# Two hyperbolic graph layers: full-row products and degree 4 against paired half-row products, degree 3 and ends from dot products

## The chip, the core and the metric

The kernel runs on one core of a Trainium2 chip. The metric is the device time of one execution in microseconds (us); lower is better. The core has five engines with a queue each: TensorE (PE, its weight loads shown apart as PEld), VectorE (DVE), ScalarE (ACT), GpSimd (POOL) and SyncE (SP, which here only issues transfers).

## What is computed

Four graph layers are applied to `x` (3327 nodes, 64 features, float32) with a dense 0/1 matrix `adj` (3327 x 3327). Each layer normalises `x` over its features, takes the positive part `h`, and adds the layer's output to `x`. Layers 0 and 3 are the hyperbolic ones, and only they change:

```python
x_t = logmap0(h, c)
left, right = x_t @ w[:64], x_t @ w[64:]
adj_att = sigmoid(left[:, None] + right[None, :] + b) * adj
x_local = logmap(h[:, None, :], h[None, :, :], c)      # all pairs of nodes
support = einsum('ij,ijd->id', adj_att, x_local)
x = x + proj(expmap(h, support, c), c)
```

`logmap` and `expmap` go through `mobius_add`, `artanh` and `tanh`; c is 1 in layer 0 and 1/r^2 in layer 3. Layer 1 is a sum over neighbours with decaying weights, layer 2 a gated recurrent unit over sums of neighbours.

## The kernel before

Nodes are padded to 3328, that is T = 26 blocks of P = 128, so `[P, T, 64]` tiles hold one row per node (1664 numbers in a partition). The order of work is layer 0, layer 1 (`plain_decay`), layer 2 (`plain_gat`), layer 3, then a branch that is taken only if the inputs leave the range for which the fast formulas hold. A tile framework puts the instructions of each engine in an order at build time, from the dependences and the number of buffers of each tile, and it sets all semaphores; each engine then runs its queue in that order.

Both hyperbolic layers are `hyperbolic_series` (L235 to L390). All pairs (j, i) are worked off as a matrix of 3328 x 3328 weights: per pair, a polynomial in a quantity L that is an inner product of two prepared rows of length 65, times the attention weight. The function has three stages.

*Preparation* (L247 to L338). DVE makes `H` by `norm_relu`, the squared norms `x2`, and `rows` (64 features and one number per node). TensorE transposes `rows` to `LT` (65 x 3328) by `to_columns` (L108: four transposes into a PSUM tile, then one ACT copy); `RT` is `LT` with signs. A chain of small operations with square root and logarithm gives the scale of `logmap0`; the scaled `H` is transposed to `xtT`; TensorE then makes `left`, spread over all partitions (`leftB`, L333), and `right` (L337).

*Pair loop* (L340 to L379). Outer loop `c`: 4 chunks of W = 832 columns i. Inner loop `b2`: 13 pairs of blocks of j. In each pass ACT makes two sigmoids (L357, 832 wide), POOL multiplies them by the adjacency (L359, 1664 wide; in layer 0 from a float32 tile that SP loads, with the diagonal taken out by `drop_diagonal`; in layer 3 from float8 masks that layer 1 left in SBUF). Then for each of the two blocks:

```python
PE.matmul(L[:, h, :BK], LT[:, b*P:(b+1)*P], RT[:, ...], ...)      # L364, h = 0, 1; 65 rows, 416 columns
A.activation(y, Lu, AF.Square, scale=0.5, bias=g1_c)              # L368
A.activation(y, y, AF.Square, bias=g2_c)                          # L369
V.scalar_tensor_tensor(Lu, Lu, 0.5 * G3, y, ...)                  # L370
V.scalar_tensor_tensor(w, Lu, G4 - 0.5 * G3, sig[...], ...)       # L372
PE.matmul(acc[h], rows[:, b, :], w[:, h, :], ...)                 # L375, h = 0, 1; 65 output rows
```

The two sums `acc[0]` and `acc[1]` (65 x 416 each) collect all 26 blocks and are copied out by ACT (L379, one buffer each) at the end of a chunk. `L` has three buffers of two PSUM banks. `sig`, `y` and `w` have two buffers.

*End* (L381 to L390). TensorE turns the sums back into rows (`to_rows`, L124), DVE copies them to `M` (L383), and `move` (L149 to L233) does `expmap`, the addition in the ball and the projection with full `[P, T, 64]` operands: `dot` is a product (L153) and a sum (L155) over 1664 numbers, `axpby` two products and an addition (L162 to L164). The last one adds to `X` (L233).

Layer 1's loop (L882 to L916) is not changed but is used below: it alternates bfloat16 matmuls over the full array (L900, L904, 128 x 128) with pairs of matmuls whose outputs are 64 columns wide and go to the two halves of the output partitions (L909).

Of the kernel before, what the change touches and what calls it, by code (L numbers as in the profile page):

```python
# [9 lines left out]
F32 = mybir.dt.float32  # L10
BF = mybir.dt.bfloat16
# [7 lines left out]
P = 128  # L19
# [9 lines left out]
G0, G1, G2, G3, G4 = 0.30970640316, -0.36098355479, 0.46940675477, -1.28660460234, 2.86920527402  # L29
X2_MIN = 18.0  # L30
# [3 lines left out]
def tile_gnn4(ctx: ExitStack, tc: tile.TileContext, x, adjT, att0, b0, w1, bias1, w_gat, a_gat,  # L34
# [26 lines left out]
    g1_c = column(G1 - 0.5, "g1_c")  # L61
    g2_c = column(G2, "g2_c")
# [172 lines left out]
    def hyperbolic_series(att, b_att, r, min_norm, min_norm2, ok, masks=None):  # L235
# [8 lines left out]
        W = 2 * BK  # L244
        R = D + 1
        with ExitStack() as st:
            pers = st.enter_context(tc.tile_pool(name="hs", bufs=1))  # L247
            rows = pers.tile([P, T, R], F32, name="rows")
# [3 lines left out]
            LT = pers.tile([R, NP], F32, name="LT")  # L252
            RT = pers.tile([R, NP], F32, name="RT")
            leftB = pers.tile([P, NP], F32, name="leftB")
            right = pers.tile([P, T], F32, name="right")
            maxn2 = pers.tile([P, 1], F32, name="maxn2")
            um = pers.tile([P, 1], F32, name="um")
            isqc = None

            with tc.tile_pool(name="hsp", bufs=1) as tp, tc.tile_pool(name="hsps", bufs=2, space=PSUM) as ps:  # L260
                w_l = tp.tile([D, 1], F32, name="w_l")
                w_r = tp.tile([D, 1], F32, name="w_r")
                nc.sync.dma_start(w_l, att[:D])
                nc.sync.dma_start(w_r, att[D:])
                bcol = tp.tile([P, 1], F32, name="bcol")
                nc.scalar.dma_start(bcol, bcast_rows(b_att))
                w_lb = tp.tile([D, P], F32, name="w_lb")
                V.tensor_copy(w_lb, w_l.to_broadcast([D, P]))
# [6 lines left out]
                floor = tp.tile([P, 1], F32, name="floor")  # L275
                V.memset(floor, 1e-7)
                V.memset(maxn2, min_norm2)
                if r is None:
                    V.memset(um, min_norm)
                    V.tensor_copy(hs, H)  # L280
                else:
# [5 lines left out]
                    isqc = pers.tile([P, 1], F32, name="isqc")  # L287
                    V.reciprocal(isqc, sqc)
                    V.tensor_scalar(um, sqc, min_norm, None, op0=OP.mult)
                    V.tensor_scalar(maxn2, cc, min_norm2, None, op0=OP.mult)  # L290
                    V.tensor_max(floor, floor, maxn2)
# [7 lines left out]
                V.tensor_mul(rows[:, :, :D], hs, wide(ia))  # L299
                V.tensor_scalar(rows[:, :, :D], rows[:, :, :D], 2.0, None, op0=OP.mult)  # L300
                V.scalar_tensor_tensor(rows[:, :, D], x2, 1.0, ia, op0=OP.add, op1=OP.mult)


                z = tp.tile([P, T], F32, name="z")
                V.tensor_scalar(z, x2, floor, None, op0=OP.max)
                z = sqrt_(tp, z, "zs")
                zc = tp.tile([P, T], F32, name="zc")
                v = tp.tile([P, T], F32, name="zv")
                lu = tp.tile([P, T], F32, name="zlu")
                lv = tp.tile([P, T], F32, name="zlv")  # L310
                V.tensor_scalar(zc, z, CLIP, None, op0=OP.min)
                V.tensor_scalar(v, zc, -1.0, 1.0, op0=OP.mult, op1=OP.add)
                A.activation(lu, zc, AF.Ln, bias=one_c)
                A.activation(lv, v, AF.Ln)
                V.scalar_tensor_tensor(v, zc, 1.0, v, op0=OP.add, op1=OP.subtract)
                V.scalar_tensor_tensor(v, zc, 2.0, v, op0=OP.mult, op1=OP.subtract)
                V.tensor_sub(lu, lu, lv)
                V.tensor_add(lu, lu, v)
                V.reciprocal(z, z)
                V.scalar_tensor_tensor(z, lu, 0.5, z, op0=OP.mult, op1=OP.mult)  # L320
                xt = tp.tile([P, T, D], F32, name="ln_sq")
                V.tensor_mul(xt, H, wide(z))

                to_columns(ps, LT, rows, R)
                sgn = tp.tile([R, 1], F32, name="sgn")
                V.memset(sgn, 1.0)
                V.memset(sgn[:D], -1.0)
                V.tensor_scalar(RT, LT, sgn, None, op0=OP.mult)
                xtT = tp.tile([D, NP], F32, name="xtT")
                to_columns(ps, xtT, xt, D)  # L330
                for k in range(NP // BK):
                    pl = ps.tile([P, BK], F32, name="pl")
                    PE.matmul(pl, w_lb, xtT[:, k * BK:(k + 1) * BK], start=True, stop=True)  # L333
                    V.tensor_copy(leftB[:, k * BK:(k + 1) * BK], pl)
                pr = ps.tile([P, T], F32, name="pr")
                for t in range(T):
                    PE.matmul(pr[:, t:t + 1], xtT[:, t * P:(t + 1) * P], w_r, start=True, stop=True)  # L337
                V.tensor_scalar(right, pr, bcol, None, op0=OP.add)  # L338

            with tc.tile_pool(name="hsw", bufs=2) as wk, tc.tile_pool(name="hsps", bufs=3, space=PSUM) as ps, \  # L340
                    tc.tile_pool(name="hsacc", bufs=1, space=PSUM) as pa:
                for c in range(NP // W):
                    c0 = c * W
                    acc = [pa.tile([R, BK], F32, name=f"acc{h}") for h in range(2)]
                    for b2 in range(T // 2):
                        if masks is None:
                            adj = wk.tile([P, 2, W], F32, name="adj", bufs=4)
# [752 lines left out]
```

## Time and profile before

| what | value |
|---|---|
| median of three runs | 1274.11 us (1266.6 to 1274.59) |
| the profiled execution: its time | 1277.46 us |
| the profiled execution: its span | 1275.7 us |
| mean granted TensorE clock | 0.895 |
| layer 0: preparation, pair loop, end | 57.7, 337.6, 50.8 us |
| layer 1 and layer 2 | 253.9 and 140.0 us |
| layer 3: preparation, pair loop, end | 49.6, 327.4, 58.7 us (the last with the store) |

A line of a stage table has the stretch, its length, the busy time of each engine with its number of instructions, the granted TensorE clock (1 is full), and the share and rate of the transfers. A line of a group has the source line, the engine, the operation, output and inputs by name, the shapes, the number of instructions, then busy time and mean ns of one, then the idle time of the engine ahead of them with what ended it. A line of a timeline has start and length in us, engine, line, operation, shapes and how many consecutive ones are merged (x4).

### The profile page before, as it was taken

Reading aid. Unit: us, or ns where it says so; the run is one execution under the profiler, and the core shown is the slowest. Engines: PE = TensorE matmul, PEld = TensorE weight load, DVE = VectorE, ACT = ScalarE, POOL = GpSimd, SP = SyncE. Lnnn points to the kernel's source line nnn. Section 1 sums busy time; section 2 is a strip of 40 time slices with the busy share of each in tenths; the row PEclk is TensorE's granted clock in tenths of the full one; section 3 lists DMA queues with packets and bytes.
Section 4 is the critical chain, followed back from the end, with each engine's and each line's share of the span. In section 5 each row is a group of like instructions: output and inputs, shape, how many; then the busy total and the mean of one; then the engine's idle time right before and its main releaser. Section 6 shows DMA issues by size and latency. Waiting matters only on the chain.

```text
span 1275.7 us, 11381 instructions
## 1 busy us (share of the span) xinstructions
PE 997.5 (78%) x4051; PEld 477.7 (37%) x4051; DVE 823.7 (65%) x937; ACT 726.2 (57%) x851; POOL 393.6 (31%) x166
## 2 busy tenths in 40 slices
PE   0989999999993037888996699919899998999910
PEld 0634444344441032333332476406344443444400
DVE  7255666566668969994933402793466676667787
ACT  1378879889883013444453001413689999899910
POOL 0065665665661000201210000000445555455500
PEclk9789989999997568999999799966799999999965
DMA  2153444444420009992910000000000000000001
GB/s 28 57 171 121 134 134 134 134 136 135 139 101 0 0 21 341 302 305 82 297 47 9 6 2 1 1 0 1 0 1 1 0 1 1 0 1 1 0 3 28
DMA packets 41844, 91.62 MB, mean 72 GB/s; under 512 B 15152, under 2 KB 15152, under 8 KB 41776
## 3 DMA queue, kind: packets, MB, share of 16 engines
q1 hardware_dynamic: 37200, 90.76, 21.9%
q10 hardware_dynamic: 4576, 0.02, 0.3%
q8 instruction: 34, 0.56, 0.2%
q14 instruction: 34, 0.28, 0.1%
HBM read 89.92 MB, written 0.85 MB: 71 GB/s over the span
## 4 chain that ended last, share of the span: by engine, by line
PE 45%; DVE 22%; ACT 17%; POOL 7%; issue 6%; DMA 2%; ACTq 0%; DVEq 0%; POOLq 0%; SPq 0%
PE acc L375 13%; PE L L364 9%; POOL sig L359 7%; PE acc L909 6%; ACT y L369 5%; DVE w L372 5%; PE acc L974 4%; ACT w L902 4%; PE cnt L904 4%; ACT sig L357 3%; ACT y L368 3%; DVE L L370 3%; PE cnt L900 2%; PE pt L114 2%; DVE prod L153 1%
## 5 line engine op out<-in xcount | busy, mean ns | idle before, releaser
L375 PE MATMUL acc<-w,rows 128*65 128x416 f32 x832 | 341.3, 535 | 39.9 <-DVE w L372 38.1
L364 PE MATMUL L<-RT,LT 65*128 65x416 f32 x832 | 334.2, 527 | 0.7 <-DVE right L338 0.7
L370 DVE SCALAR_TENSOR_TENSOR L<-L,y 128x832 f32<-128x832 f32 x208 | 213.8, 1030 | 185.4 <-ACT y L369 181.7
L359 POOL TENSOR_TENSOR sig<-mask,sig 128x1664 f32<-128x1664 fp8e4 x52 | 164.6, 3167 | 385.2 <-ACT sig L357 375.1
L372 DVE SCALAR_TENSOR_TENSOR w<-L,sig 128x832 f32<-128x832 f32 x208 | 212.5, 1024 | 52.9 <-POOL sig L359 35.8
L368 ACT ACTIVATE y<-L,g_c 128x832 f32<-128x832 f32 x208 | 195.8, 943 | 76.5 <-PE L L364 76.5
L359 POOL TENSOR_TENSOR sig<-adj,sig 128x1664 f32<-128x1664 f32 x52 | 193.1, 3716 | 102.2 <-ACT sig L357 102.1
L364 PEld LDWEIGHTS L<-RT,LT 65*128 65x128 f32 x832 | 162.6, 196 | 149.9 <-issue 146.9
L369 ACT ACTIVATE y<-y,g_c 128x832 f32<-128x832 f32 x208 | 203.9, 983 | 3.5
L357 ACT ACTIVATE sig<-leftB,right 128x832 f32<-128x832 f32 x208 | 201.2, 977 | 7.5 <-DVE w L372 7.4
L375 PEld LDWEIGHTS acc<-w,rows 128*65 128x65 f32 x832 | 108.9, 141 | 242.7 <-DVE w L372 117.1
L902 ACT ACTIVATE w<-cnt,ebias 128x832 bf16<-128x832 f32 x104 | 93.7, 950 | 110.9 <-PE cnt L900 68.8
L146 POOL TENSOR_TENSOR mask<-mask,offdiag 128x128 fp8e4<-128x128 fp8e4 x26 | 23.4, 902 | 248.0 <-PE cnt L904 241.6
L895 DVE SCALAR_TENSOR_TENSOR same<-adj 128x1664 bf16<-128x1664 f32 x52 | 99.0, 1904 | 0.0
L909 PE MATMUL acc<-w,sup 128*64 128x416 bf16 x624 | 94.0, 349 | 0.0
L904 PE MATMUL cnt<-mask,rest 128*128 128x416 fp8e4 x208 | 54.1, 341 | 28.7 <-ACT w L902 28.7
L900 PE MATMUL cnt<-mask,after 128*128 128x416 fp8e4 x208 | 55.2, 350 | 9.7 <-DVE mask L892 9.7
L974 PE MATMUL acc<-mask,h 128*64 128x416 fp8e4 x624 | 60.9, 345 | 0.7 <-ACT hP L827 0.7
L909 PEld LDWEIGHTS <-sup 128*64 128x64 bf16 x624 | 38.1, 110 | 49.9 <-issue 37.0
L892 DVE TENSOR_SCALAR mask<-adj 128x1664 fp8e4<-128x1664 f32 x52 | 54.9, 1056 | 1.1 <-DMA adj<-in 1.1
L114 PE MATMUL pt<-ident,rows 128*65 128x128 f32 x52 | 12.0, 426 | 54.4 <-DVE zs L86 30.2
L114 PE MATMUL pt<-ident,H 128*64 128x128 f32 x26 | 5.3, 366 | 61.4 <-DVE H L106 61.4
(247 smaller groups left out, 657.9 us busy)
## 6 DMA issues: line engine op xcount, KB each, us to landing
adj<-in SPq DMA_DIRECT2D x104, 832.0 KB, 4.8
X<-in SPq DMA_DIRECT2D x1, 832.0 KB, 7.8
out<-X SPq DMA_DIRECT2D x1, 832.0 KB, 6.0
gw<-in SPq DMA_DIRECT2D x8, 48.0 KB, 2.3
gb<-in ACTq DMA_DIRECT2D x8, 0.8 KB, 2.0
w_l<-in SPq DMA_DIRECT2D x2, 0.2 KB, 5.2
bcol<-in ACTq DMA_DIRECT2D x2, 0.5 KB, 5.4
w_r<-in SPq DMA_DIRECT2D x2, 0.2 KB, 4.1
```

What stands on the lines that cost most here:

```text
L357: A.activation(sig[:, s, :], leftB[:, c0:c0 + W], AF.Sigmoid, bias=right[:, b:b + 1])
L359: G.tensor_tensor(sig, adj, sig, op=OP.mult)
L364: PE.matmul(L[:, h, :BK], LT[:, b * P:(b + 1) * P], RT[:, c0 + h * BK:c0 + (h + 1) * BK], start=True, stop=True)
L368: A.activation(y, Lu, AF.Square, scale=0.5, bias=g1_c)
L369: A.activation(y, y, AF.Square, bias=g2_c)
L370: V.scalar_tensor_tensor(Lu, Lu, 0.5 * G3, y, op0=OP.mult, op1=OP.add)
L372: V.scalar_tensor_tensor(w, Lu, G4 - 0.5 * G3, sig[:, s, :].rearrange("p (h i) -> p h i", h=2), op0=OP.add, op1=OP.mult)
L375: PE.matmul(acc[h], rows[:, b, :], w[:, h, :], start=(b == 0), stop=(b == T - 1))
L902: A.activation(w[:, o, :, :], cnt[o][:, :, :BK], AF.Exp, scale=-LN2, bias=ebias)
L904: PE.matmul(cnt[o][:, h, :BK], rest, mask[:, o, h * BK:(h + 1) * BK], start=False, stop=True, skip_group_check=True)
L909: PE.matmul(acc[h][o * D:(o + 1) * D, :], parts[k][:, b, :], w[:, o, h, :], start=first and k == 0, stop=last and k == 2)
L974: PE.matmul((acc[k] if i < 3 else cnt[k])[o * D:(o + 1) * D, :], w, mask[:, o * HP + k * BK:o * HP + (k + 1) * BK], start=b == 0 and i in ...
```

## The change

Only `hyperbolic_series` changes, with the constants of its polynomial. In words:

- **Polynomial.** Degree 3 in place of 4. One `Square` on ACT (with L shifted and scaled), one `scalar_tensor_tensor` and one `tensor_mul` on DVE.
- **Tiling of the pair loop.** 512 columns in place of 832: six chunks of 512 and one of 256; still 13 pairs of blocks in each. One `L` tile holds both blocks of a pair (2 x 512, two banks); ACT's square and both DVE operations do the whole tile, 1024 wide; the sigmoids are 512 wide, POOL's product 1024.
- **Products.** The 64 features of `rows` are laid out twice in `XT`, in partitions 0 to 63 and 64 to 127. The inner product of the first block of a pair reads the upper half, that of the second the lower half, each with 64 rows, in float32. The 65th term and the constant come from a second, bfloat16 matmul of 9 rows per block (`ET`, `FT`: numbers cut into three bfloat16 parts), at partitions 0 and 32, that adds to the same PSUM bank.
- **Sums.** One matmul of 512 columns per block into one accumulator of 65 x 512, with two buffers. At the end of each chunk ACT copies it out, TensorE transposes it in an `L` tile, and ACT copies that into `M`.
- **left.** No longer kept for all columns: per chunk, a matmul with a 0/1 matrix (`pick`) spreads it, and DVE copies it (`leftB`, 512 wide).
- **Preparation.** The logarithms go (`artanh` is taken at its clip). `left` and `right` are products and sums on DVE. `XT` takes a transpose and a float32 matmul with the identity per block; `E` and `F`, `[P, T, 64]` tiles, are filled by small operations and transposed to `ET` and `FT`. The copy to `hs` in layer 0 goes to ACT.
- **End.** `move` is replaced: everything lies in the plane of `hs` and `Mx`, so two dot products (`hm`, `mm`) and operations on `[P, T]` numbers (26 in a partition) give two coefficients per node, and the result is `X + ah*hs + am*Mx`.

```diff
-G0, G1, G2, G3, G4 = 0.30970640316, -0.36098355479, 0.46940675477, -1.28660460234, 2.86920527402
-X2_MIN = 18.0
+G0, G1, G2, G3 = -0.3851200397, -1.4315723663, 0.0289761757, 1.8129648238
+X2_MIN = 22.0
...
-        W = 2 * BK
-        R = D + 1
+        W = 512
+        NF = 12
...
+            XT = pers.tile([P, NP], F32, name="XT")
+            ET = pers.tile([D, NP], BF, name="ET")
+            FT = pers.tile([D, NP], BF, name="FT")
+            pick = pers.tile([NF, P], BF, name="pick")
...
+                for t0 in range(0, T, 4):
+                    n = min(4, T - t0)
+                    pt = ps.tile([P, 4 * P], F32, name="pt")
+                    for k in range(n):
+                        PE.transpose(pt[:D, k * P:(k + 1) * P], rows[:, t0 + k, :D], ident)
+                        PE.matmul(pt[D:, k * P:(k + 1) * P], rows[:, t0 + k, :D], ident, start=True, stop=True)
+                    A.activation(XT[:, t0 * P:(t0 + n) * P], pt[:, :n * P], AF.Copy)
+                p0 = parts3(x0, "p0")
...
+                for k, o in ((0, left), (1, right)):
+                    sq = tp.tile([P, T, D], F32, name="ln_sq")
+                    V.tensor_mul(sq, H, wlr[:, k, None, :].to_broadcast([P, T, D]))
+                    V.reduce_sum(o, sq, axis=AX.X)
+                    V.tensor_mul(o, o, z)
...
+                for dst, src in ((ET, E), (FT, F)):
+                    to_columns(ps, dst, src, D)
...
+            with tc.tile_pool(name="hsw", bufs=3) as wk, tc.tile_pool(name="hsps", bufs=3, space=PSUM) as ps, \
+                    tc.tile_pool(name="hsacc", bufs=2, space=PSUM) as pa:
+                for c0 in range(0, NP, W):
+                    n = min(W, NP - c0)
+                    cs = slice(c0, c0 + n)
+                    acc = pa.tile([D + 1, W], F32, name="acc")
+                    Ll = ps.tile([P, 2, W], F32, name="L")
+                    PE.matmul(Ll[:, 0, :n], pick, FT[:NF, cs], start=True, stop=True)
+                    leftB = wk.tile([P, W], F32, name="leftB", bufs=2)
+                    V.tensor_copy(leftB[:, :n], Ll[:, 0, :n])
...
+                        G.tensor_tensor(sig, adj, sig, op=OP.mult)
+                        L = ps.tile([P, 2, W], F32, name="L")[:, :, :n]
+                        blocks = [slice((2 * b2 + s) * P, (2 * b2 + s + 1) * P) for s in range(2)]
+                        for s in range(2):
+                            q = slice(s * D, (s + 1) * D)
+                            PE.matmul(L[:, s, :], XT[q, blocks[s]], XT[q, cs], start=True, stop=False)
+                        for s in range(2):
+                            e = slice(s * 32, s * 32 + 9)
+                            PE.matmul(L[:, s, :], ET[e, blocks[s]], FT[e, cs], start=False, stop=True)
+                        y = wk.tile([P, 2, W], F32, name="y", bufs=2)[:, :, :n]
+                        A.activation(y, L, AF.Square, scale=-0.5, bias=shift_c)
+                        V.scalar_tensor_tensor(L, y, G3, L, op0=OP.add, op1=OP.mult)
+                        w = wk.tile([P, 2, W], F32, name="w")[:, :, :n]
+                        V.tensor_mul(w, L, sig)
                         for s in range(2):
                             b = 2 * b2 + s
-                            A.activation(y, Lu, AF.Square, scale=0.5, bias=g1_c)
-                            A.activation(y, y, AF.Square, bias=g2_c)
...
+                            PE.matmul(acc[:, :n], rows[:, b, :], w[:, s, :], start=b == 0, stop=b == T - 1)
+                    a = wk.tile([D + 1, W], F32, name="sum", bufs=2)
+                    A.activation(a[:, :n], acc[:, :n], AF.Copy)
+                    t0, nt = c0 // P, n // P
+                    Lm = ps.tile([P, 2, W], F32, name="L")[:, 0, :nt * (D + 1)].rearrange(
+                        "p (t d) -> p t d", d=D + 1)
+                    for k in range(nt):
+                        PE.transpose(Lm[:, k, :], a[:, k * P:(k + 1) * P], ident[:D + 1, :D + 1])
+                    A.activation(M[:, t0:t0 + nt, :], Lm, AF.Copy)
...
+                hm = dot(hs, Mx, "hm")
+                mm = dot(Mx, Mx, "mm")
...
+                for a, b in ((hs, ah), (Mx, am)):
+                    prod = tp.tile([P, T, D], F32, name="prod", bufs=2)
+                    V.tensor_mul(prod, a, wide(b))
+                    V.tensor_add(X, X, prod)
```

Between `mm` and the last loop there are, in layer 0, some 58 operations of DVE on `[P, T]` tiles and two of ACT (a tanh and a square root); in layer 3 there is one more square root.

## The prediction

> **What bounds the kernel now.** I read the stage table first.
>
> ```profile
> 57.70:395.30 337.60, 314.61 (x835) 136.61 (x836) 210.91 (x208) 285.39 (x320) 204.40 (x80) 0.96 0.41 132
> 395.30:446.10 50.80, 1.96 (x27) 1.66 (x25) 48.83 (x59) 5.04 (x7) 0.00 (x0) 0.56 0.00 0
> 840.00:889.60 49.60, 26.30 (x121) 20.12 (x121) 32.51 (x66) 11.06 (x22) 0.00 (x0) 0.60 0.01 0
> 889.60:1217.00 327.40, 310.52 (x841) 135.81 (x842) 212.55 (x210) 284.96 (x321) 164.62 (x52) 0.96 0.00 1
> ```
>
> The pair loops are 665 of 1276 us, and in them TensorE is busy for 93% and 95%, ScalarE for 85%. The ends are VectorE alone (48.83 of 50.80). Then the groups of layer 3's loop:
>
> ```profile
> L375 PE MATMUL acc<-w,rows 128*65 128x416 f32 x416 | 169.6, 533 | 16.9 <-DVE w L372 15.9 <-ACT RT L379 0.3
> L364 PE MATMUL L<-RT,LT 65*128 65x416 f32 x416 | 166.7, 526 | 0.3 <-DVE right L338 0.3
> L359 POOL TENSOR_TENSOR sig<-mask,sig 128x1664 f32<-128x1664 fp8e4 x52 | 164.6, 3167 | 385.2 <-ACT sig L357 375.1
> ...
> L370 DVE SCALAR_TENSOR_TENSOR L<-L,y 128x832 f32<-128x832 f32 x104 | 107.0, 1031 | 94.8 <-ACT y L369 94.7
> L372 DVE SCALAR_TENSOR_TENSOR w<-L,sig 128x832 f32<-128x832 f32 x104 | 106.2, 1024 | 18.4 <-POOL sig L359 9.8 <-PE acc L375 1.4
> ```
>
> The code asks for 208 products at each of these PE lines, and the trace has 416: a float32 matmul is two instructions. The timeline has their price, and ScalarE's:
>
> ```profile
> 1025.12 0.98 ACT L357 ACTIVATE sig<-leftB,right 128x832 f32<-128x832 f32 x1
> 1025.46 1.56 PE L364 MATMUL L<-RT,LT 65*128 65x416 f32 x4
> ...
> 1025.99 0.98 ACT L369 ACTIVATE y<-y,g_c 128x832 f32<-128x832 f32 x1
> ...
> 1026.86 1.61 PE L375 MATMUL acc<-w,rows 128*65 128x416 f32 x4
> ```
>
> Four instructions start to start take 1.40 us, 0.35 each, and nothing is lost from L364 to L375. So a loop is 832 x 0.349 = 290 us of TensorE at full clock; it takes 337.6 and 327.4. The excess of 47 and 37 us is the half clock at the start (8.7 and 6.9 us for the first two dozens of instructions, in place of 4.2 each), filling, and waits among queues that are nearly all full: ScalarE starts one per 0.88 us, 312 x 0.88 = 275 us. Last, a stretch of layer 1, where the shape of the array in use changes:
>
> ```profile
> 644.32 1.24 PE L909 MATMUL acc<-w,sup 128*64 128x416 bf16 x10
> 645.50 0.53 PE L900 MATMUL cnt<-mask,after 128*128 128x416 fp8e4 x2
> 645.95 0.54 PE L909 MATMUL acc<-w,sup 128*64 128x416 bf16 x2
> ```
>
> A full-array bfloat16 matmul of 416 columns is 0.175 us. Ten half-width ones take 1.18 us to the next start where five times 0.175 would be 0.88: they run in twos, and leaving them costs 0.30. The two of L900 take 0.45 for 0.35: entering costs 0.10.
>
> **The change, part by part.** *Ends.* Now 50.8 us from the last sum to the last addition in both layers. After: 8 operations 1664 wide (two products, two sums, two products, two additions) at 1.89 = 15.1; some 57 small ones behind each other at 0.20 (row: 0.18 long, 0.21 apart; the independent ones closer) = 11.4; five reciprocals 0.14 more each, 0.7; two round trips to ScalarE, 1.0; last sum to `M`, 1.5. That is 30 us in layer 0 and 31.5 in layer 3 (another square root, with its table load of 1.28 us). Gain 21 + 19.5 = 40. No work covers either.
>
> *Preparation.* Now 57.7 and 49.6 us, of which 27 are TensorE's transposes and products behind `rows`. VectorE's chain gets longer: `left` and `right` are four wide operations, 7.6; small pieces for `E` and `F` about 40 at 0.15 to 0.2, 7; gone are `RT`, the `hs` copy or the doubling (1.0 to 2.0 each). It ends near 45 us where it began at 8.5. TensorE has 26 transposes with 52 extra float32 instructions for `XT` (seven groups at about 1.8, estimated from 0.92 for a group of four transposes), `E` (7 x 0.92) beside VectorE, and `F` behind it (first group 0.92, all 6.4). The loop can start at 50 to 54: gain 5 per layer. Bounds: 0 (all of `F` and the spreading matmul in the way) to 9 (VectorE's chain alone).
>
> *ScalarE, VectorE, POOL in the loop.* Per full pass (2 x 512 columns; 78 of them per layer and 13 half ones). ScalarE: 0.88 is 832 wide; 192 more at 0.9 ns (603 ns for 416 against 977 for 832) give 1.05 for the square, 320 fewer give 0.59 for a sigmoid: 2.23 us, 188 per layer with the half ones, for 275. VectorE: 1.03 + 192 x 1.06 ns = 1.23, twice, 2.47: 209 per layer, as now. POOL: 3.72 x 1024/1664 = 2.3 in layer 0, 200 and 12 for the diagonals; 2.0 in layer 3. None is near a pass of TensorE. If TensorE had no cost, VectorE would be the bound.
>
> *TensorE in the loop.* 0.349 us for 416 columns is 0.43 for 512. The sums: 4 x 0.43 = 1.72. The bfloat16 correction: 0.175 x 512/416 = 0.215 each. The two half-row products: four instructions of 0.43, in the order of the code two of the first product and then two of the second. No row of this trace has two float32 matmuls side by side; L909 shows that halves of the array overlap in bfloat16. Bounds: side by side wholly 0.86, not at all 1.72. I take 1.29: the second part of the first product must follow its first in the same rows, so only the middle two overlap. The correction is 0.215 in a pair (0.43 if not). Sum 1.29 + 0.215 + 1.72 = 3.22.
>
> To this come the changes of shape, three per pass (full, 64 rows, 9 rows, full), none now. L909 and L900 give 0.10 for entering a smaller shape and 0.30 for leaving: 0.50 per pass. Bounds 0 and 0.9. The Trainium skill speaks against the change here (TensorEngine Tiling (Array Packing), Key Properties): a change of tiling mode drains TensorE. It gives no figure; the rows above agree with it. Without drains the sum at the end would be 91 us lower (182 passes of 0.5), 1139; with them it is as given.
>
> A pass is then 3.72, a half one 2.11: 78 x 3.72 + 13 x 2.11 = 318 per layer. Of the present excess I keep 18: 7 for the cold start, 5 for filling, 6 for seven chunk changes. There `pick` takes a turn of `L`, and the sigmoids of the new chunk wait behind VectorE's copy of it (0.6); the transposes of the sum take another, and the next products queue behind them while ScalarE copies the sum out (0.5). The other 19 to 29 come from waits among queues that are 90% full beside TensorE; with ScalarE at 60% of it they should go; kept whole, they are the upper end. Loop: 336, that is -2 in layer 0 and +8 in layer 3.
>
> The page TensorE: Matmul & The Clock Gate (The mechanism) has row tiles starting about 4 ns apart; read so, the pair would cost 0.86, and the sum would be that of rival 1. Its own rule that matmuls start in program order is what I follow; no run here shows either for float32.
>
> *Transfers.* In layer 0 SP issues 91 loads of the adjacency in place of 52, with the same bytes in all; the loop's transfers take 0.41 of the transfer engines now, and four buffers hide a landing of 4.8 us: nothing. Without that cover a pass would wait the 4.8 us, more than a pass of 3.72.
>
> *Sum.* 1277.5 (the profiled execution) - 40 - 10 + 6 = 1233.5; the median is 3.4 lower than that execution, so 1230.
>
> **Rivals.**
> 1. *Pairs overlap wholly, or shapes change for little.* The product pair 0.86: pass 3.30, half 1.90, 282 + 18 = 300 per layer: 1230 - 72 = 1158. With free changes of shape too, 2.80: 255 per layer, 1068. The floor is VectorE, 209 + 18: 1012. For it: L909's pairs. Against: two instructions per product.
> 2. *Float32 halves don't overlap: slower.* Product 1.72, correction 0.43, pass 4.37, half 2.44: 373 + 18 = 391 per layer, +110: 1340. The point where it decides: to the time of now there are 44 us, over 91 passes twice 0.24 us per pass. Any price of shapes above 0.74 does as much with overlap. For it: no row shows float32 pairs. Against: nothing in L909 depends on the type.
> 3. *The cover is spent elsewhere.* Preparation gains nothing (+10), and half to all of the 19 + 29 us of waits stay (+24 to +48): 1264 to 1288, no change. For it: half the preparation runs at clock 0.60. Against: ScalarE's load falls by a third.
>
> **How the numbers follow.** Forecast (1200 to 1260, from shape changes of 0.35 to 0.65 per pass) 0.47; rival 1 0.27; rival 2 0.15; rival 3 0.11. The measurement tells 1% from no change. Below 1261: the forecast and rival 1, 0.74. Within 1%: 0.11. Above 1287: 0.15. The range leaves out the lower third of rival 1 and the upper part of rival 2: 1135 to 1300.
>
> **What would show it.** Right: ends of about 30 us; ScalarE's share in the loop near 57%, POOL's and VectorE's near 62%; PE's L instructions starting 0.43 apart but for one pair that starts together; gaps of 0.1 to 0.3 us on PE at each change of rows, three per pass; a pass of 3.7 us. Wrong: all four product instructions in 0.86 us (rival 1), or 1.72 in a row (rival 2); gaps of PE that end on VectorE or POOL, which would mean that another engine has become the bound; a granted clock below 0.9 in the loops, since pauses in the ends go with 0.56 (stage table) and would make every term of TensorE longer.

## The result and the profile after

The changed kernel takes 1330.19 us (median of four runs, 1324.05 to 1333.29), the kernel before 1272.13 us on the same chip. The ratio is 1.0457, with a 95% interval of 1.0401 to 1.0512: the change makes the kernel slower by 4 to 5%. The forecast was 1230 us, with a range of 1135 to 1300. The profiled execution of the changed kernel took 1328.02 us, with a span of 1326.3. Beside the experiments below the kernel before took 1270.25 to 1271.5 us, so that their medians can be set against each other.

The stage table of the kernel after, with the columns of the one shown before (stretch, length, busy time of each engine, granted clock, transfers):

```profile
0.00:65.30 65.30, 33.89 (x133) 16.19 (x133) 34.40 (x80) 14.70 (x25) 4.56 (x13) 1.00 0.12 15
65.30:432.70 367.40, 327.61 (x941) 93.62 (x940) 212.20 (x189) 209.19 (x287) 209.97 (x117) 0.97 0.40 121
432.70:458.70 26.00, 0.34 (x2) 0.20 (x2) 23.73 (x70) 2.38 (x5) 0.00 (x0) 0.55 0.00 0
458.70:854.10 395.40, 316.00 (x2093) 156.03 (x2093) 240.85 (x280) 124.26 (x156) 25.63 (x26) 0.91 0.34 114
854.10:916.50 62.40, 34.61 (x131) 16.71 (x131) 33.35 (x83) 13.28 (x25) 5.10 (x5) 0.55 0.01 1
916.50:1290.30 373.80, 339.06 (x941) 95.58 (x940) 212.37 (x189) 208.95 (x286) 171.16 (x91) 0.94 0.00 0
1290.30:1326.30 36.00, 0.54 (x5) 0.29 (x4) 23.65 (x69) 5.18 (x8) 0.00 (x0) 0.53 0.11 26
```

| stage | before | after | difference | forecast |
|---|---|---|---|---|
| layer 0: preparation | 57.7 | 65.3 | +7.6 | -5 |
| layer 0: pair loop | 337.6 | 367.4 | +29.8 | -2 |
| layer 0: end | 50.8 | 26.0 | -24.8 | -21 |
| layers 1 and 2 | 393.9 | 395.4 | +1.5 | 0 |
| layer 3: preparation | 49.6 | 62.4 | +12.8 | -5 |
| layer 3: pair loop | 327.4 | 373.8 | +46.4 | +8 |
| layer 3: end and store | 58.7 | 36.0 | -22.7 | -19.5 |

The ends gain what they should and a little more. The loops and the preparations, which were to change by -4 us in all, take 97 us more. The groups of layer 3's loop say who waits in it:

```profile
L408 PE MATMUL acc<-w,rows 128*65 128x512 f32 x312 | 161.0, 641 | 28.2 <-DVE w L405 28.2
L391 POOL TENSOR_TENSOR sig<-mask,sig 128x1024 f32<-128x1024 fp8e4 x78 | 156.9, 2018 | 231.9 <-ACT sig L389 202.5 <-DVE L L403 29.4
L396 PE MATMUL L<-XT 64*128 64x512 f32 x312 | 129.2, 690 | 0.0
...
L403 DVE SCALAR_TENSOR_TENSOR L<-y,L 128x1024 f32<-128x1024 f32 x78 | 95.7, 1228 | 114.1 <-ACT y L402 114.1
...
L402 ACT ACTIVATE y<-L,shift_c 128x1024 f32<-128x1024 f32 x78 | 86.3, 1107 | 73.4 <-PE L L399 73.4
```

VectorE waits 114 us for ScalarE's square, and that square 73 us for TensorE's products, so TensorE is still the bound, as forecast; but it stands still in front of the sums for 28 us (before: 16.9 us in front of L375), and the stretch has a granted clock of 0.94. The timeline of TensorE in that loop shows what a pass is made of:

```profile
1003.55 1.93 PE L408 MATMUL acc<-w,rows 128*65 128x512 f32 x4
1005.41 1.12 PE L396 MATMUL L<-XT 64*128 64x512 f32 x2
1006.47 0.39 PE L399 MATMUL L<-FT,ET 9*128 9x512 bf16 x2
1006.78 1.93 PE L408 MATMUL acc<-w,rows 128*65 128x512 f32 x4
1008.65 1.13 PE L396 MATMUL L<-XT 64*128 64x512 f32 x4
1009.71 0.39 PE L399 MATMUL L<-FT,ET 9*128 9x512 bf16 x2
1010.02 1.12 PE L396 MATMUL L<-XT 64*128 64x512 f32 x2
```

Read the starts. Four product instructions, both blocks of a pass, take 1.06 us to the next start (1008.65 to 1009.71). Two instructions, one block alone, take 1.06 us as well (1005.41 to 1006.47). Sums take 1.86, the two corrections 0.31. So a pass whose two products stand next to each other takes 1.06 + 0.31 + 1.86 = 3.23 us, and one whose products are torn apart, with the sums of an earlier pass between them, 4.29. The scheduler tears 5 of 13 pairs in each full chunk and 7 of 13 in the half one. This is its order for a full chunk (K spreads `left`, P product, C correction, A sum, T transpose of the sums):

```
K PP CC PP CC PP CC AA P AA P AA CC PP CC PP AA CC P AA P CC AA PP CC P AA P CC AA
PP CC P AA P CC AA PP CC P AA P CC AA AA TTTT
```

The end of that chunk, in layer 0 (the last column has idle time of the engine ahead of the instruction, and what ended it):

```profile
174.15 1.93 PE L408 MATMUL acc<-w,rows 128*65 128x512 f32 x4 [1.94 <-DVE w L405]
176.77 0.46 PE L415 MATMUL L<-ident,sum 65*128 65x65 f32 x4 [0.68 <-ACT sum L410]
177.16 0.38 PE L375 MATMUL L<-FT,pick 12*128 12x512 bf16 x1
177.48 1.13 PE L396 MATMUL L<-XT 64*128 64x512 f32 x4
...
181.30 0.39 PE L399 MATMUL L<-FT,ET 9*128 9x512 bf16 x2
183.97 1.93 PE L408 MATMUL acc<-w,rows 128*65 128x512 f32 x4 [2.28 <-DVE w L405]
```

TensorE stops three times: for the `w` of the last pass, since the products of the next chunk stand behind the transposes in its queue; for ScalarE's copy of the sums; and for the first `w` of the new chunk. That is 4.9 us. The last of the three is a chain: VectorE's copy of `left` starts at 177.59, three sigmoids at 178.37, the square at 180.23, VectorE's two operations at 181.35 and 182.69, the sums at 183.97. A fourth pause, of 1.36 us, stands inside every full chunk of layer 0, in front of the sums after the sixth product pair (141.22 in this one).

The passes of a full chunk are worth 8 x 3.23 + 5 x 4.29 = 47.3 us, but chunks of layer 0 start 57.6, 54.6, 56.1, 56.5, 54.6 and 54.7 us apart. So a chunk costs 7.3 us beyond its passes at full clock, and up to 9.2 here; the first one, with 10.3, has the start of the loop in it, and the average is 8.4. In layer 3 the starts are 57.1 us apart on average, 9.8 beyond the passes.

### The profile page after: what moved, and what is told of

The parts are those of the page before. It is cut to its first block, busy times and chain, and to the rows that moved or that the text cites. A ratio compares the mean times of both kernels' runs of the same rounds, so it can differ in the third digit from the quotient of the medians.

```text
span 1326.3 us, 11639 instructions
## 1 busy us (share of the span) xinstructions
PE 1052.0 (79%) x4241; PEld 378.6 (29%) x4241; DVE 780.5 (59%) x958; ACT 577.9 (44%) x791; POOL 416.4 (31%) x252
## 5 line engine op out<-in xcount | busy, mean ns | idle before, releaser
L408 PE MATMUL acc<-w,rows 128*65 128x512 f32 (+1 forms) x728 | 344.9, 598 | 66.3 <-DVE w L405 66.3
L403 DVE SCALAR_TENSOR_TENSOR L<-y,L 128x1024 f32<-128x1024 f32 (+1 forms) x182 | 209.5, 1151 | 242.0 <-ACT y L402 242.0
L396 PE MATMUL L<-XT 64*128 64x512 f32 (+1 forms) x728 | 281.3, 639 | 0.0
L389 ACT ACTIVATE sig<-leftB,right 128x512 f32<-128x512 f32 (+1 forms) x364 | 233.8, 682 | 89.4 <-DVE w L405 80.4
L402 ACT ACTIVATE y<-L,shift_c 128x1024 f32<-128x1024 f32 (+1 forms) x182 | 190.4, 1046 | 157.1 <-PE L L399 157.1
L391 POOL TENSOR_TENSOR sig<-mask,sig 128x1024 f32<-128x1024 fp8e4 (+1 forms) x91 | 171.2, 1887 | 254.1 <-ACT sig L389 224.6
L391 POOL TENSOR_TENSOR sig<-adj,sig 128x1024 f32<-128x1024 f32 (+1 forms) x91 | 199.1, 2201 | 140.8 <-ACT sig L389 120.5
L405 DVE TENSOR_TENSOR w<-L,sig 128x1024 f32<-128x1024 f32 (+1 forms) x182 | 209.1, 1149 | 22.6 <-POOL sig L391 3.2
L396 PEld LDWEIGHTS L<-XT 64*128 64x128 f32 x728 | 78.7, 192 | 128.5 <-issue 120.6
L1045 PE MATMUL cnt<-mask,rest 128*128 128x416 fp8e4 x208 | 54.6, 344 | 28.8 <-ACT w L1043 28.8
L399 PE MATMUL L<-FT,ET 9*128 9x512 bf16 (+1 forms) x364 | 69.3, 377 | 0.0
L1041 PE MATMUL cnt<-mask,after 128*128 128x416 fp8e4 x208 | 55.8, 352 | 10.3 <-DVE mask L1033 10.3
```

Source lines behind the costliest of these rows:

```text
L389: A.activation(sig[:, s, :], leftB[:, :n], AF.Sigmoid, bias=right[:, 2 * b2 + s:2 * b2 + s + 1])
L391: G.tensor_tensor(sig, adj, sig, op=OP.mult)
L396: PE.matmul(L[:, s, :], XT[q, blocks[s]], XT[q, cs], start=True, stop=False)
L399: PE.matmul(L[:, s, :], ET[e, blocks[s]], FT[e, cs], start=False, stop=True)
L402: A.activation(y, L, AF.Square, scale=-0.5, bias=shift_c)
L403: V.scalar_tensor_tensor(L, y, G3, L, op0=OP.add, op1=OP.mult)
```

## The experiments

The theory after the traces (A): three separate losses, the torn pairs, the chunk changes and the identity products in the preparation; the float32 halves do overlap. The rivals: (B) for the order, that a pass is bound by its changes of shape, whatever the order, and for the chunk changes, that they cost no more than the 6 us of the forecast; (C) the preparation is bound by VectorE, so TensorE's work there doesn't count; and the forecast's own rival 2, float32 halves that don't overlap. The letters of the later expectations are their own.

**e1_order: TensorE's order pinned inside a chunk.**

```diff
-                            PE.matmul(L[:, s, :], XT[q, blocks[s]], XT[q, cs], start=True, stop=False)
+                            pin(PE.matmul(L[:, s, :], XT[q, blocks[s]], XT[q, cs], start=True, stop=False))
...
+                        late.append((w, b2))
+                        if len(late) == 3:
+                            sums(acc, n, *late.pop(0))
```

`pin` keeps an instruction in the order of the program. Corrections, sums, transposes and the spread of `left` are pinned in the same way, and `sums` issues the sums of the pass two earlier.

> TensorE's order written by hand within a chunk (products and corrections of a pass together, the sums two passes later); nothing else. Theory A (a product pair overlaps when its two halves stand side by side in the queue, and the planner's order tore 37 of 91 pairs per layer apart at 1.06 us each, 0.63 in the half chunk): 30 x 1.06 + 7 x 0.63 = 36 us per layer less, about 1258. Rival B (a pass is bound by the changes of shape, whatever the order): no change, 1325 to 1335.

Measured: 1223.52 us, 0.962 of before (0.9579 to 0.9662). B falls: the product pairs stand together, and a pass takes 3.24 us.

```profile
92.45 1.93 PE L379 MATMUL acc<-w,rows 128*65 128x512 f32 x4
94.31 1.13 PE L407 MATMUL L<-XT 64*128 64x512 f32 x4
95.38 0.39 PE L410 MATMUL L<-FT,ET 9*128 9x512 bf16 x2
95.69 1.93 PE L379 MATMUL acc<-w,rows 128*65 128x512 f32 x4
```

It gains 107 us where A expected 72. In layer 0's loop it is 48 (319.1 us for 367.4): the torn pairs make 36 of them (30 at 1.06, seven half ones at about 0.6), and the chunk changes get shorter too. Full chunks start 48.9 us apart on average where 13 x 3.24 = 42.1 are work, so a change costs 6.8 us and not 8.4, and the half chunk loses less. Layer 3's loop, where the clock of the changed kernel is lower, gains 55 (318.8 for 373.8; granted clock 0.96 for 0.94). The edit does two things, it keeps pairs together and it sets the sums two passes back; e10_all_torn, below, keeps the second and undoes the first.

**e2_chunks: nothing at the end of a chunk but one copy.** The sums go to an SBUF tile and are turned into rows after the loop, as in the kernel before; `left` is spread for all columns in the preparation.

```diff
-                    Ll = ps.tile([P, 2, W], F32, name="L")
-                    PE.matmul(Ll[:, 0, :n], pick, FT[:NF, cs], ...)
...
-                    a = wk.tile([D + 1, W], F32, name="sum", bufs=2)
+                    A.activation(ST[:, cs], acc[:, :n], AF.Copy)
...
+                to_rows(ps, ST, D + 1, lambda t0, n, src: V.tensor_copy(M[:, t0:t0 + n, :], src))
```

> Chunk changes relieved: the sums stay in SBUF and are turned into rows after the loop, and the spread of left is made for all columns in the preparation. Theory A (at each chunk change TensorE's queue waits for ScalarE's copy of the sum and for the last weights, runs dry, and comes back at half clock, about 8.8 us over 13 passes): six changes per layer, 53 us, less about 6 for what moves to the preparation and the end: 1330 - 94 = 1236. Rival B (nothing lost there beyond the 6 us per loop of the prediction): 1325 to 1340.

Measured: 1252.66 us, 0.9849 (0.9775 to 0.9923); 17 above the expectation of A, far below B's. The scheduler now tears 44 of 91 pairs in place of 37, which is about 15 us. With that, layer 0's loop is 325.0 us, of which the passes are 321 (78 x 3.23 + 13 x 1.86, and 44 torn): the chunk changes are gone almost wholly.

**e12_left: only the spread of `left` moved.** The half of e2_chunks' edit that takes `left` out of the chunk changes; the transposes stay.

> The changed kernel with only the spread of left moved out of the chunk changes (made for all columns in the preparation); the sums are still copied and transposed at the end of each chunk, and as many pairs are torn per chunk as in the changed kernel (5 of 13). e2_chunks moved both; this tells which of the two costs. The spreading in the preparation costs about 4.4 us per layer (first product 69.7 for 65.3 in e2_chunks). If the sigmoids that wait for leftB cause the last pause of a change (2.28 us in front of the first sums of a chunk): 14 changes at 2.3 and some half clock less, about 35 us off, 9 added: 1304. If the whole change hangs on the transposes of the sum: 1339. By the prediction's price for leftB (0.6 per change): 8 off, 9 added, 1331.

Measured: 1292.7 us, 1.0177 (1.0144 to 1.0211): 37 us off where 26 were expected. The pauses of a change are 1.26, 0.68 and 1.42 us in place of 1.94, 0.68 and 2.28:

```profile
172.31 1.93 PE L410 MATMUL acc<-w,rows 128*65 128x512 f32 x4 [1.26 <-DVE w L407]
174.93 0.46 PE L417 MATMUL L<-ident,sum 65*128 65x65 f32 x4 [0.68 <-ACT sum L412]
...
180.63 1.93 PE L410 MATMUL acc<-w,rows 128*65 128x512 f32 x4 [1.42 <-DVE w L407]
```

and in layer 0 its chunks from the second to the fifth are alike, at full clock; two of them:

```profile
123.00:175.10 52.10, 48.06 (x137) 13.00 (x136) 31.80 (x26) 31.54 (x41) 31.03 (x16) 1.00 0.43 131
175.10:227.20 52.10, 48.07 (x137) 13.01 (x137) 31.81 (x26) 31.54 (x41) 31.85 (x16) 1.00 0.44 132
```

Those of the changed kernel are not:

```profile
122.50:177.20 54.70, 48.43 (x138) 13.12 (x136) 32.32 (x27) 31.45 (x41) 30.40 (x13) 1.00 0.41 125
177.20:233.20 56.00, 49.19 (x136) 13.21 (x135) 32.32 (x27) 31.46 (x41) 32.10 (x17) 0.98 0.41 122
233.20:289.70 56.50, 51.93 (x136) 13.71 (x135) 32.32 (x27) 31.46 (x41) 32.06 (x17) 0.93 0.40 121
```

So the loss at a change has a second part: after pauses of about 2 us TensorE came back at half clock in some of the chunks, which makes 54.7 into 56.1 and 56.5 here, and up to 60.1 in layer 3. Shorter pauses make this rarer and do not rule it out: in layer 3 of e12_left the clock halved twice after a pause of 1.42 us, once here:

```profile
1065.83 3.45 PE L410 MATMUL acc<-w,rows 128*65 128x512 f32 x4 [1.42 <-DVE w L407]
```

**e3_prep: the features doubled in `rows`, one full transpose per block.**

```diff
+                A.activation(rows2[:, :, :D], rows[:, :, :D], AF.Copy)
-                        PE.transpose(pt[:D, k * P:(k + 1) * P], rows[:, t0 + k, :D], ident)
-                        PE.matmul(pt[D:, k * P:(k + 1) * P], rows[:, t0 + k, :D], ident, ...)
+                        PE.transpose(pt[:, k * P:(k + 1) * P], rows2[:, t0 + k, :2 * D], ident)
```

> Preparation: rows hold the features twice, so one full transpose per block gives both halves of XT, in place of a transpose and a float32 product in two shapes. Theory A (a block takes 0.97 us in the trace after, with two changes of shape, 25 us per layer on the path): about 7 us in place of 25, 1330 - 36 = 1294. Rival C (the preparation waits for VectorE's chain, so TensorE's part is hidden): 1325 to 1332.

Measured: 1301.19 us, 1.0231 (1.0188 to 1.0274). C falls: the first product starts at 46.9 us in place of 65.3. In the kernel after a block alternates a transpose and two matmuls,

```profile
53.24 0.42 PE L336 MATMUL pt<-ident,rows 128*64 128x128 f32 x1
53.60 0.69 PE L337 MATMUL pt<-ident,rows 128*64 128x128 f32 x2
54.21 0.42 PE L336 MATMUL pt<-ident,rows 128*64 128x128 f32 x1
```

0.97 us per block, 25.3 for 26; in e3_prep 24 of them take 5.2:

```profile
31.50 5.16 PE L338 MATMUL pt<-ident,rows 128*128 128x128 f32 x24 [31.50 <-ACT rows L331]
```

Layer 3's preparation is shorter by 19 us too. That 37 us of preparation gave 29 in all has its reason in the loop of layer 0: with as many torn pairs, its six full chunks took 344.1 us in place of 334.1, at a lower clock (0.89 to 0.94, for 0.93 to 1.00). One of them:

```profile
105.30:165.40 60.10, 53.84 (x136) 14.08 (x136) 32.31 (x27) 31.45 (x41) 30.36 (x13) 0.89 0.39 114
```

**e4_same_rows: both products read partitions 0 to 63.** The same work, all of it on one half of the rows.

```diff
-                            q = slice(s * D, (s + 1) * D)
+                            q = slice(0, D)
```

> Both half-row products read partitions 0 to 63 (same numbers, same result), so they cannot lie beside each other. Theory A (54 of 91 pairs per layer stand together and overlap wholly): 48 x 0.86 + 6 x 0.43 = 44 us per layer more, 1418. The prediction's view (only the middle two of four instructions overlap): 48 x 0.43 + 6 x 0.21, 22 us per layer, 1374. Rival 2 of the prediction (no overlap in float32): 1330.

Measured: 1432.92 us (one run; before 1271.37), 15 above what A expected, with a granted clock of 0.873 for 0.906. The pair that stands together now takes 1.91 us to the next start, not 1.06:

```profile
1000.47 1.98 PE L396 MATMUL L<-XT 64*128 64x512 f32 x4
1002.38 0.39 PE L399 MATMUL L<-FT,ET 9*128 9x512 bf16 x2
```

Four float32 instructions with no change of shape take 1.72 us (e6_full_rows, below, 205.90 to 207.62), so about 0.20 is for leaving the shape, and of the 1.06 there remain 0.86 for four: float32 halves overlap wholly. Rival 2 of the forecast is wrong, though its time, 1340, is the nearest to the result.

**e10_all_torn: the sums pinned between the products.** As e1_order, with 77 of 91 pairs torn.

> As e1_order, but the sums of two passes earlier are pinned between the two products of a pass, in 11 of 13 passes of every chunk (77 of 91 per layer; e1_order has none, the changed kernel 37). If a torn pair costs 1.06 us, as the timeline of the changed kernel has it: 65 full passes at 1.06 and 12 half ones at about 0.6, 76 per layer, 152 over e1_order: 1376. If tearing costs nothing and the gain of e1_order came from somewhere else in the order (sums two passes later): as e1_order, 1223.

Measured: 1447.37 us, 1.1392 (1.135 to 1.1433). The same work in another order of TensorE's queue takes 224 us more than in e1_order, the lower clock that came with it included (0.871 for 0.908). A torn pass is 4.29 us, 1.05 above e1_order's, as expected. The expectation still misses 71 us. Some 47 of them are in the half chunks, which ran at half clock from end to end, 57.2 us where some 34 were due:

```profile
441.80:499.00 57.20, 55.17 (x134) 22.55 (x131) 18.37 (x27) 19.91 (x41) 17.24 (x15) 0.53 0.15 42
```

The rest, some 25, is in the full chunks, which start 13.8 us further apart than e1_order's, not the 11.7 of eleven torn pairs. After a pause of 1.29 us that ended at 445.75 TensorE worked there for 50 us with no pause, and the clock did not come back. Why is open.

**e5_all: the three edits together, with TensorE's order pinned across chunks.**

> The three edits of the order of the queue, the sums kept to the end of the loop and the doubled rows in one kernel; TensorE's order is pinned across the whole loop (products and corrections of a pass, then the sums of two passes earlier), so no chunk change has a pause. Theory A (the three losses are separate: torn pairs, pauses at chunk changes, the identity products of the preparation): pass 3.24 us as measured in e1_order, half pass 1.86, so 277 + 12 for start and tail = 289 per loop; preparations 51 and 48; ends 28 and 38 with the store; layers 1 and 2 397: 1140 (1125 to 1155). Rival B (a denser TensorE is given a lower clock: 0.87 in place of 0.91, as in e4_same_rows): 26 us more on the loops, 1165. Rival C (order and chunk changes are one and the same loss, so only the larger counts): e1_order's 1223 less the preparation's 29, 1195.

Measured: 1149.3 us, 0.9053 (0.9021 to 0.9084). The losses are separate (A), nearly: 9 us are missing. The lower clock (its B) did not come, 0.923 is granted, and the one common loss (its C) is out by 46. The missing part is in every second pass, where TensorE waits 0.26 us for VectorE, and ScalarE's timeline shows why:

```profile
204.93 0.72 ACT L406 ACTIVATE sig<-leftA,right 128x512 f32<-128x512 f32 x1 [1.13 <-DVE w L422]
205.56 1.09 ACT L419 ACTIVATE y<-L,shift_c 128x1024 f32<-128x1024 f32 x1
206.56 0.71 ACT L406 ACTIVATE sig<-leftA,right 128x512 f32<-128x512 f32 x1
207.17 1.10 ACT L419 ACTIVATE y<-L,shift_c 128x1024 f32<-128x1024 f32 x1
```

A sigmoid for a later pass waits 1.13 us for VectorE's `w`, which frees a buffer of `sig`, and the square behind it, whose `L` is ready, waits with it.

**e9_sig4: a fourth buffer for `sig`.**

> As e5_all with four buffers for sig in place of three. In e5_all's timeline every second pass pauses 0.26 to 0.33 us in front of the sums (pass 3.24 and 3.57 in turn): a sigmoid stands in ScalarE's queue ahead of the square and waits 1.13 us for a sig buffer that VectorE's product frees. If that is the whole cause, the pauses go: 0.15 per pass over 91 passes twice is 27 us, 1122. If the next limit is close (the three buffers of L, freed by the same product of VectorE), part of it stays: 1135. If the pauses come from VectorE's own order: as e5_all, 1149.

Measured: 1148.58 us, 0.9044 (0.9028 to 0.906), nothing gained. The scheduler used the buffer to run one sigmoid further ahead; the wait of 1.13 us stayed. So the number of buffers of `sig` was not the cause, and the expectation of 1122 missed; the order of ScalarE's queue is left.

**e11_act_order: ScalarE's queue by hand.**

```diff
+                    pin(A.activation(y, L, AF.Square, scale=-0.5, bias=shift_c))
+                    if k + 2 < len(todo):
+                        sigs.append(attn(*todo[k + 2]))
```

`attn` makes the two sigmoids of a pass, pinned, and POOL's product; the rest is e9_sig4.

> As e9_sig4 with ScalarE's queue fixed by hand: the square of pass k, then the two sigmoids of pass k + 2. In e9_sig4 the fourth buffer changed nothing: the sigmoid ahead of the square still waits 1.13 us for VectorE's product, since the scheduler put three sigmoids and one in turn between the squares. If that order is what delays every second square by about a microsecond and TensorE by 0.33, the pauses go: 0.15 per pass, 27 us, 1122. If the chain from products to sums (square, two operations of VectorE, three buffers of L) is too long by itself, the pause stays whatever ScalarE's order: 1149.

Measured: 1120.91 us, 0.8825 (0.8802 to 0.8849). TensorE has no pause in a pass left:

```profile
203.26 1.93 PE L387 MATMUL acc<-w,rows 128*65 128x512 f32 x4
205.13 1.13 PE L422 MATMUL L<-XT 64*128 64x512 f32 x4
206.19 0.39 PE L425 MATMUL L<-FT,ET 9*128 9x512 bf16 x2
206.50 1.93 PE L387 MATMUL acc<-w,rows 128*65 128x512 f32 x4
```

This is the fastest version of the study that leaves nothing out, 12% below the kernel before; layer 0's loop takes 279.4 us, of which 277 are passes.

**e6_full_rows: what the pairing is worth.** e5_all with one float32 matmul of 66 rows per block and no correction.

> As e5_all, but the products take 66 full rows (64 features, the 65th term, the constant) in one float32 matmul per block, with no half rows and no bfloat16 correction; the tile E and its transposes go, a multiplication by signs comes. No change of shape is left in the loop. By the runs (pair 0.86, changes of shape about 0.44 per pass) the full rows cost 3.44 per pass for 3.24: 16 us per layer more, less some 5 per layer in the preparation: 20 to 30 us above e5_all, about 1165. By the prediction's prices (pair 1.29, changes 0.50, pass 3.72) the full rows would save 0.28 per pass: some 45 us below e5_all with the preparation, about 1095. The sign decides.

Measured: 1162.26 us, 0.9134 (0.9104 to 0.9164): 13 above e5_all, 41 above e11_act_order. The sign is that of the runs' prices. A pass is 3.44 us and TensorE never waits:

```profile
205.90 1.88 PE L399 MATMUL L<-RT,LT 66*128 66x512 f32 x4
207.62 1.88 PE L374 MATMUL acc<-w,rows 128*65 128x512 f32 x4
```

The half rows in pairs with their correction and their changes of shape save 0.20 us of 3.44 per pass, and only if the queues are in order: with ScalarE's order of e5_all (3.24 and 3.57 in turn, 3.41 on average) they save almost nothing in the loop. Layer 0's loop takes 297.9 us here, 293.7 in e5_all and 279.4 in e11_act_order.

**e7_before_new_ends: the new ends alone, in the kernel before.**

> The kernel before with only the new end of both layers (dot products in the plane), its loop and preparation as they were. If the ends gain by themselves what the trace of the changed kernel shows (26.1 and 27.6 us for 50.8 and 50.9): 48 us, about 1224. By the prediction's sum of the ends: 40 us, about 1232. If the gain was tied to the sums being already in rows (M filled in the loop), less: about 1236, since to_rows stays in this kernel at 4 to 6 us per layer.

Measured: 1225.27 us, 0.9662 (0.961 to 0.9713), 46 us off. From the last sum to the last addition to `X` layer 0 takes 27.8 us (389.6 to 417.4) for 50.8. The end's gain does not depend on the rest.

**e8_no_correction: e5_all without the bfloat16 correction.** It leaves out the 65th term and the constant, so its weights are those of another polynomial.

> As e5_all without the bfloat16 correction (the 65th term and the constant are left out of L, so the weights are those of another polynomial); everything else stays. It prices two of the four small instructions and one change of shape per pass. From the timelines: 0.31 to 0.32 us per pass, 27 per layer, 54 in all: about 1086. By the prediction's prices (0.215 and a third of 0.50): 0.38 per pass, 66 in all, about 1074. If another engine had become the bound in e5_all: as e5_all.

Measured: 1068.57 us, 0.8403 (0.8377 to 0.8429), 81 us below e5_all where 54 were expected. A pass is 2.92 us with no pause, for 3.41: 0.32 is the correction itself, the rest is e5_all's pause, which goes with it. In its trace ScalarE's queue alternates a square (202.82) with two sigmoids (203.83), the order that e11_act_order sets by hand. I had set TensorE's work against a pass in which it also waits.

## Why the prediction was wrong

*The ends: right, a little small.* Forecast 30 and 31.5 us, measured 26.0 and 27.6, a gain of 47.5 for 40. Independent small operations follow each other closer than the 0.20 that I took for all of them (0.10 us apart at 1310.13 and 1310.23, in layer 3's end). e7_before_new_ends shows the gain by itself.

*The preparation: wrong in sign.* The step that failed is "seven groups at about 1.8" for `XT`, with a loop that starts at 50 to 54. A group takes 3.9 us. I had costed transposes at the row of 26 transposes in a run, and the extra matmuls as if they came in a run too; alternating, the three instructions of a block take 0.97 us, where 24 full transposes in a row take 0.22 each. TensorE, and not VectorE, set the start. The gain of 10 was a loss of 20 (7.6 + 12.8).

*The pass: right for the wrong reasons.* Forecast 3.72 us, measured 47.3 / 13 = 3.64 on average. The product pair is 0.86, not 1.29 ("only the middle two overlap" failed: e4_same_rows); the changes of shape are 0.20 + 0.10 + 0.14 = 0.44 (estimates: 1.06 less 0.86, 0.31 less 0.215, 1.86 less 1.72), near the 0.50 from layer 1's rows; and the torn pairs add 0.41, which no term of the sum held. That 3.64 lies near 3.72 is luck: a term too large and a term left out cancel. The 0.215 came from rows of L900 that the prediction calls bfloat16; their moving operand is fp8e4, and no run separates it from the 0.10. The Trainium skill, page TensorE: Matmul & The Clock Gate (The mechanism), has row tiles start almost together; the runs agree with it also for float32, and I had weighed it and chosen against it. The rule of its page TensorEngine Tiling (Array Packing), Key Properties, that a change of mode drains TensorE, agrees with these 0.44. A torn product pays 0.20 of them once more and shares its 0.86 with nobody.

*The excess: the step that failed most.* "Of the present excess I keep 18", with 6 for seven chunk changes. Measured: 367.4 - 312 = 55 in layer 0 and 373.8 - 312 = 62 in layer 3 (the 312 are six chunks of 47.3 and about 28.5 for the half one). The prediction had named both places and mis-sized them: 0.6 for sigmoids that wait behind the copy of `left`, 0.5 for products that queue behind the transposes, about 0.9 per change in the sum. A chunk costs 7.3 us beyond its passes at full clock, eight times that: the wait for `left` goes on through sigmoids, square and VectorE to the first `w` (2.28), TensorE's queue has nothing ready while the last `w` is made (1.94) and while the sums are copied (0.68), and 1.36 are lost inside the chunk. With the half clock after the pauses, for which the sum had no term, and with the start of the loop it is 8.4 on average in layer 0 and 9.8 in layer 3. In all the excess is 81 us over the forecast in the two layers, the preparation 30. e2_chunks takes the excess to 4 us; e12_left shows that the spread of `left` alone makes some 46 us of the two layers' changes (the 37 that it gains and the 9 that it costs in the preparations).

*ScalarE off the path: true by rate, not by order.* 2.23 us per pass against TensorE's 3.24 would seem free, but in e5_all a wait in its queue holds the square, and TensorE with it; e11_act_order gains 28 us from the order alone.

*Transfers, layers 1 and 2:* as forecast, nothing.

*The rivals.* Rival 1's mechanism, whole overlap, held, and its time is out by 172; rival 2's time is 10 off, and its mechanism is refuted. Rival 3, a preparation that gains nothing and waits that stay, names the two places where the time went, but its price was 34 to 58 and the two cost 30 and 70 more than forecast. None had the order of TensorE's queue as its subject. Of the signs of being wrong, one came but did not mean what was said of it: gaps of TensorE that end on VectorE (28.2 us in layer 3's loop) were to show another engine as the bound, but VectorE is busy for 57% of that loop, and another order of TensorE's queue takes 55 us out of it (e1_order). The granted clock in the loops stayed above 0.9, at 0.97 and 0.94.

## What to carry to other kernels

Two matmuls that share the array by halves are worth their overlap only while they stand next to each other in the queue: look at the order that a scheduler has built before you price the pair, and pin it where it matters (107 us here, from order alone). Price the end of a chunk from a trace of TensorE's queue, instruction by instruction, with whatever stands behind a waiting one; a longer list of shorter chunks pays it each time. And an engine at 70% of the bound is free only if the instruction that the bound needs is not queued behind one that waits.

## What the runs showed of the hardware

- Float32 half-row products, two instructions each, overlap wholly: 0.86 us for four of 512 columns, and 1.06 to the next start of another shape, for one product or two alike.
- In the loops half clock came at chunk changes, in some chunks and not in others with the same pauses (54.6 to 60.1 us per chunk, granted clock 1.00 to 0.89). The record of the clock tells the difference: in layer 0's loop it is halved from 73.6 to 77.0, 230.6 to 237.4, 285.2 to 288.6 and 401.2 to 408.0, always for 3.4 or 6.8 us, and the starts are 157.0, 54.6 and 116.0 us apart, whole multiples of 3.41. So the clock seems to change on a grid of steps of 3.41 us. At the change of 230.6 the pause of 1.94 us lay whole in the step before (the first line); at the change before that one, 1.55 of it lay in one step (the third line), and the clock stayed:

```profile
227.20:230.60 3.40, 1.46 (x4) 0.47 (x4) 2.03 (x2) 0.00 (x0) 0.00 (x0) 1.00 0.00 0
230.60:234.00 3.40, 2.72 (x9) 0.83 (x9) 0.12 (x1) 0.98 (x2) 0.00 (x0) 0.50 0.00 0
172.60:176.00 3.40, 1.85 (x4) 0.47 (x4) 1.40 (x2) 0.00 (x0) 0.00 (x0) 1.00 0.00 0
```

- That fits a clock that is set by where a pause lies against the grid, but the pause is not the whole rule: the clock also halved after a step with 1.42 us of pause (e12_left, 1062.7 to 1066.1) and after one with none (e4_same_rows, 189.7 to 193.1, TensorE busy for 3.40 of 3.40). What else counts is open. The page TensorE: Matmul & The Clock Gate of the Trainium skill (What's actually happening) has the clock halved after an idle window of about 3.4 us; the pauses of a change were shorter than that, and here the measurement decides.
- In e10_all_torn the half clock stayed for 50 us of work without a pause, in both half chunks. No run tells why.
- A transpose that alternates with a two-instruction float32 matmul to the other half of the output partitions costs 0.97 us per block, against 0.22 for a full transpose in a row of them.
